# Layer 3's parameters in ten steps, one a unit; the state's product first in its output tile; attention begins beside the first sequence's parameters

## The chip, the core and the metric

The kernel runs on one core of a Trainium2 chip. A core has engines that each work through their own queue in order: TensorE (PE; its weight loads are shown apart as PEld), VectorE (DVE), ScalarE (ACT), GpSimd (POOL) and SyncE (SP). Matrix products go from SBUF into PSUM, from where VectorE and ScalarE read them. The metric is the time of one execution on the device in microseconds (us). Times are stated as medians over runs, and the profile shows one execution.

## The reference

The program is a stack of four layers on x of shape (8, 512, 128). Each layer computes `x = x + s * silu(g)`, with an "attention" part s and a "feed-forward" part g, both of the normalized x. Only layer 3 is changed. Its s is a state-space mixer with rotary angles, and its g an attention of 16 heads of width 8 whose softmax runs over the queries:

```python
xn = _layernorm(x, axis=-1)
# s: state-space mixer
z, x, Bg, Cg, dd_dt, dd_A, trap, angles = split(u @ W_in)
a = jnp.minimum(-softplus(dd_A), -A_FLOOR)
dt = softplus(dd_dt + dt_bias)
theta = jnp.cumsum(angles[:, :, None, :] * dt[..., None], axis=1)
K = _rope(_rmsnorm(Bg, B_norm_w)[:, :, None, :] + B_bias, theta)
Q = _rope(_rmsnorm(Cg, C_norm_w)[:, :, None, :] + C_bias, theta)
...
y = (y_intra + y_inter) + D[None, None, :, None] * x
s = (y * silu(z)).reshape(b, L, D_INNER) @ W_out
# g: attention
scores = jnp.einsum('bqd,bkd->bkq', q, k) / jnp.sqrt(D)
attn = jax.nn.softmax(scores, axis=-1)
z = _l2_normalize(jnp.einsum('bkq,bkv->bqv', attn, v) @ Wo)
g = gelu(_l2_normalize(z @ Wff))
x = x + s * silu(g)
```

`y_intra` is what a chunk of the sequence gives to itself, `y_inter` what the state before the chunk gives to it.

## The kernel before

Layer 3 works on 8 sequences of 512 tokens, each in JT = 4 tiles of 128 tokens. All of a sequence's work is written as Python generators, each `yield` ending one step:

- `begin(b)`: layernorm, transposed tokens xT, the projections kT, qT, V, and then `parameters`.
- `parameters(q)`: B, C, dt, decay, angles and so on for the whole sequence. It holds the products L1743 to L1747, two tanh, `softplus` (a chain of some 15 small VectorE operations on 128x32 elements, L1608 to L1620), the decay's sums L1777 with their exponentials L1779, the norm of B and C (`rms` and L1789), their dot products, and theta (L1808 and L1810) with its reduction to one turn and sine and cosine (L1815 to L1828).
- `mixer(b, jt)`: one tile of the state-space mixer: z and x (L1838), rotation (L1852 to L1854), decay matrix E (L1859, L1864), transposes of B and C into kqT (L1878, copied out by L120 on ScalarE or L122 on VectorE in turn), their products (L1883) times E (L1884), the new state (L1889 to L1895), then the output tile `py` with both halves: the chunk's own product (L1900), read by VectorE at L1901, and the state's (L1904), read at L1906. The sum times z (L1909) is transposed into `yT` (L1913).
- `scores(b, u)`: one unit, four heads by 128 keys: four products into four PSUM banks `pu` (L1946), four maxima on VectorE (L1949), four exponentials with their sums on ScalarE (L1950). `weigh(b, u)`, two units later (LAG = 2), scales the values (L1923, and L1924 on POOL) and adds the products up in one bank `pf` (L1931).
- `end(b)`: W_out's product s (L1959), Wo's product z (L1969), the norms, Wff (L1985), Gelu, the gate and the output's DMA (L1997).

`layer3` sets the order. `begin(0)` runs to its end first. Then follow 8 x 16 units and LAG more; in each unit `scores` and `weigh` are emitted with higher priority (AHEAD = 300), and every generator that is running makes one step, half of them between `scores` and `weigh`. `begin(b + 1)` starts with sequence b's unit 0, a mixer four units ahead of the unit with its number (HEAD = 4), `end(b)` right after the last weigh.

TensorE's instructions keep the order in which they are written (`manual_schedule`). Those of the other engines are ordered by a scheduler, by priority and readiness, when the program is built; each engine then runs its own in that order. All products but scores and weigh go through a ring of three PSUM tiles `pa`. A tile may be written anew when all that read its last contents are done, and a tile is tracked as a whole: a write to one half of `py` waits for reads of the other.

Of the kernel before, what the change touches and what calls it, by code (L numbers as in the profile page):

```python
# [10 lines left out]
F32 = mybir.dt.float32  # L11
# [9 lines left out]
P = 128  # L21
B = 8
T = 512
C = 128
N = B * T
NT = N // P
JT = T // P
H = 16
LAG = 2
# [1533 lines left out]
HM, HP = 4, 64  # L1563
# [40 lines left out]
def softplus(nc, pool, x):  # L1604

    shape = list(x.shape)
    tl = lambda name: pool.tile(shape, F32, name=name)
    e, z, q, p = tl("sp_e"), tl("sp_z"), tl("sp_q"), tl("sp_p")  # L1608
    nc.scalar.activation(e, x, AF.Abs)
    nc.scalar.activation(e, e, AF.Exp, scale=-1.0)  # L1610
    nc.vector.tensor_scalar(z, e, 2.0, None, ALU.add)
    nc.vector.reciprocal(z, z)
    nc.vector.tensor_tensor(z, z, e, ALU.mult)
    nc.vector.tensor_tensor(q, z, z, ALU.mult)
    nc.vector.tensor_scalar(p, q, 1.0 / 17, None, ALU.mult)
    for n in range(15, 1, -2):
        nc.vector.scalar_tensor_tensor(p, p, 1.0 / n, q, ALU.add, ALU.mult)
    nc.vector.scalar_tensor_tensor(p, p, 1.0, z, ALU.add, ALU.mult)
    nc.vector.tensor_scalar(x, x, 0.0, None, ALU.max)
    nc.vector.scalar_tensor_tensor(x, p, 2.0, x, ALU.mult, ALU.add)  # L1620


class Layer3:
# [69 lines left out]
    def begin(self, b):  # L1693
# [32 lines left out]
        q["oT"] = tp.tile([P, 4, T], F32, name="oT3", bufs=1)  # L1726
        q["held"], q["po"] = {}, {}
        yield
        yield from self.parameters(q)

    def parameters(self, q):
# [20 lines left out]

        beta = sm("beta3", 2, JT, HM)
        nc.scalar.activation(beta[:, 0], par[:, :, 8:12], AF.Tanh, scale=0.5)
# [47 lines left out]

        nc.vector.tensor_tensor(v["coef"], v["coef"], kqd, ALU.mult)
# [23 lines left out]
        nc.scalar.activation(n, n, AF.Square)  # L1827
        nc.vector.tensor_scalar(of(cos), n, -2.0, 1.0, ALU.mult, ALU.add)  # L1828
        q.update(v=v, BC=BC, sin=sin, cos=cos, state=None)
        q["yT"] = tp.tile([P, 2, JT, P], F32, name="yT3", bufs=1)  # L1830

    def mixer(self, b, jt):

# [62 lines left out]
            q["state"] = new  # L1896
        yield
        py = k.pa((P, 2, HM, HP))
        for h in range(HM):
            nc.tensor.matmul(py[:, 0, h, :], E[:, h, :], xc[:, h, :], start=True, stop=True)  # L1900
        nc.vector.tensor_tensor(y, y, py[:, 0], ALU.add)  # L1901
        if state is not None:
            for h in range(HM):
                nc.tensor.matmul(py[:, 1, h, :], kqT[:, 1, h, :], state[:, h, :], start=True, stop=True)  # L1904
# [12 lines left out]
    def weigh(self, b, u):  # L1917
# [34 lines left out]
    def end(self, b):  # L1952

        k, nc, cn, fn, tp, q = self.k, self.k.nc, self.cn, self.fn, self.tp, self.q.pop(b)
        s = tp.tile([P, JT, C], F32, name="s3", bufs=1)
        ps = k.pa((P, JT, C))
        for jt in range(JT):
            for w in range(2):
                nc.tensor.matmul(  # L1959
                    ps[:, jt, :], q["yT"][:, w, jt, :], cn["W_out"][:, w * C : (w + 1) * C],  # L1960
                    start=(w == 0), stop=(w == 1),
                )
        nc.scalar.copy(s, ps)
        yield
        z = tp.tile([P, JT, C], F32, name="zo3", bufs=1)
        ps = k.pa((P, JT, C))
        for qt in range(JT):
# [4 lines left out]
                )  # L1972
        nc.scalar.copy(z, ps)
        yield
        r = self.rms(z, JT, 1e-12, floor=True)
        nc.vector.tensor_tensor(z, z, bc(r, 2, C), ALU.mult)
        yield
# [23 lines left out]
def layer3(k, x, A, at):  # L2001

    with ExitStack() as ctx:
        ctx.enter_context(k.banks("l3p", pu=4, pf=1, pa=3))
        L = Layer3(k, ctx, x, A, at, k.out)
        ctx.enter_context(k.tc.manual_schedule(engines={mybir.EngineType.PE}))
        for _ in L.begin(0):
            pass
        U = 4 * JT
        AHEAD = 300  # L2010
        HEAD = 4
        running = [L.mixer(0, 0)]
        for n in range(B * U + LAG):
            b, u = divmod(n, U)
            steps = iter(running)

            def step(share):

                for _ in range(share):
                    w = next(steps, None)  # L2020
                    if w is not None and next(w, False) is False:
                        running.remove(w)

            if b < B:
                if u == 0 and b + 1 < B:
                    running.append(L.begin(b + 1))
                mb, mu = divmod(n + HEAD, U)
                if mb < B and mu % 4 == 0 and (mb, mu) != (0, 0):
                    running.append(L.mixer(mb, mu // 4))
                steps = iter(list(running))  # L2030
                half = (len(running) + 1) // 2
                with k.tc.high_priority(offset=AHEAD):
                    L.scores(b, u)
                step(half)
            else:
                half = 0
            if n >= LAG:
                wb, wu = divmod(n - LAG, U)
                with k.tc.high_priority(offset=AHEAD):
                    L.weigh(wb, wu)  # L2040
                if wu == U - 1:
                    running.insert(0, L.end(wb))
            step(len(running))
        while running:
            for w in list(running):
                if next(w, False) is False:
# [87 lines left out]
```

## Time and profile before

| | us |
|---|---|
| median of 3 timed runs (lowest, highest) | 3675.19 (3669.09, 3679.26) |
| the profiled execution's own time | 3659.7 |
| its span, first to last instruction | 3658.0 |
| first and last start of a reduction L1949 | 2689.6 and 3630.0 |

Layer 3's constants are loaded at 2646.5 us, so it takes the last 1011 us of the span. Start of the first reduction of each sequence's unit 0, from the trace: 2689.6, 2813.8, 2935.5, 3055.6, 3178.1, 3296.4, 3416.9 and 3534.1 us, that is 117 to 124 us a sequence, and 94 for the last up to its last exponential.

The page gives each engine's busy time, share of the span and instructions, and then the span in 40 slices (91 us each), one digit for the busy tenths of each:

```profile
PE 2812.2 (77%) x16390; PEld 1510.1 (41%) x16390; DVE 2265.6 (62%) x6274; ACT 1643.1 (45%) x3211; POOL 783.7 (21%) x915
...
PE   6164657512988888699999999998668789887987
...
DVE  7989898997581121334445445444467777777775
ACT  5163546512544445233333333333245566666665
...
PEclk8585757555899999799998998998878899888987
```

The last eleven slices are layer 3. PEclk is the TensorE clock that was granted, in tenths of full speed. Of the costliest groups, these belong to layer 3 (line, engine, operation, out<-in with shapes, count; busy us and mean ns of one; idle time of the engine just before, and what ended it):

```profile
L1950 ACT ACTIVATE at<-pu,nm 128x512 f32<-128x512 f32 x512 | 347.7, 687 | 145.9 <-DVE nm L1949 115.6
...
L1949 DVE TENSOR_REDUCE nm<-pu 128x1 f32<-128x512 f32 x512 | 326.4, 679 | 66.8 <-PE pu L1946 66.7
...
L1946 PE MATMUL pu<-qT,kT 32*128 32x512 f32 x1024 | 247.6, 700 | 6.4 <-ACT at L1950 5.4
```

A matmul of this kind is recorded as two instructions, and four matmuls on different rows of the array run at once.

### The profile page before, as it was taken

How to read it: one execution, taken by the hardware profiler on the slowest of the kernel's cores; microseconds unless marked ns; L12 is line 12 of the kernel's file. 1: busy time of each engine (PE TensorE's matmuls, PEld its weight loads, DVE VectorE, ACT ScalarE, POOL GpSimd, SP SyncE). 2: the span in 40 equal slices, each digit the busy share in tenths (PEclk: the TensorE clock that was granted, in tenths of full speed). 3: DMA queues.
4: the chain of work that ended last, by engine and by line, in shares of the span. 5: the costliest groups of instructions: out<-in, count | busy, mean ns of one | idle time of the engine just before them, and what ended most of it. 6: DMA issues, size and time to landing. Idle time of an engine off the chain costs nothing.

```text
span 3658.0 us, 45079 instructions
## 1 busy us (share of the span) xinstructions
PE 2812.2 (77%) x16390; PEld 1510.1 (41%) x16390; DVE 2265.6 (62%) x6274; ACT 1643.1 (45%) x3211; POOL 783.7 (21%) x915
## 2 busy tenths in 40 slices
PE   6164657512988888699999999998668789887987
PEld 4142445302444444344444444444344445444543
DVE  7989898997581121334445445444467777777775
ACT  5163546512544445233333333333245566666665
POOL 0004040400226664201101101101122222222220
PEclk8585757555899999799998998998878899888987
DMA  4002030311002221100000000000000000000000
GB/s 119 2 2 71 1 81 1 72 48 34 1 10 45 38 38 24 58 1 1 1 1 1 1 1 1 1 1 1 18 3 1 4 4 1 4 4 4 1 4 6
DMA packets 67519, 64.53 MB, mean 18 GB/s; under 512 B 5344, under 2 KB 59616, under 8 KB 66784
## 3 DMA queue, kind: packets, MB, share of 16 engines
q1 hardware_dynamic: 39264, 42.75, 3.7%
q0 software_dynamic: 19712, 14.69, 2.9%
q10 hardware_dynamic: 8320, 4.19, 0.4%
q8 instruction: 129, 2.11, 0.2%
q14 instruction: 94, 0.77, 0.1%
HBM read 43.80 MB, written 17.83 MB: 17 GB/s over the span
## 4 chain that ended last, share of the span: by engine, by line
PE 45%; DVE 32%; ACT 13%; POOL 4%; issue 3%; DMA 1%; ACTq 0%; POOLq 0%; SPq 0%; DVEq 0%
PE pa L1361 6%; PE pu L1379 6%; DVE nm L1949 4%; ACT at L1950 4%; PE pu L1066 2%; PE pf L1086 2%; PE pu L1946 2%; DVE mpad L1393 2%; PE pf L1424 2%; DVE Z L700 2%; PE pf L1931 1%; PE pa L1475 1%; PE pa L1474 1%; PE pa L1000 1%; DVE Z L706 1%
## 5 line engine op out<-in xcount | busy, mean ns | idle before, releaser
L1950 ACT ACTIVATE at<-pu,nm 128x512 f32<-128x512 f32 x512 | 347.7, 687 | 145.9 <-DVE nm L1949 115.6
L199 POOL TENSOR_SCALAR_AFFINE_SELECT at<-at 128x512 f32<-128x512 f32 x256 | 187.2, 751 | 1030.4 <-ACT at L1411 856.9
L1949 DVE TENSOR_REDUCE nm<-pu 128x1 f32<-128x512 f32 x512 | 326.4, 679 | 66.8 <-PE pu L1946 66.7
L1393 DVE TENSOR_REDUCE mpad<-pu 128x2 f32<-128x256 f32 (+3 forms) x256 | 199.0, 817 | 169.1 <-PE pu L1390 169.1
L1411 ACT ACTIVATE at<-pu 128x1024 f32<-128x1024 f32 (+3 forms) x256 | 171.6, 701 | 286.3 <-PE pu L1379 286.1
L1071 ACT ACTIVATE at<-pu,rsqrt 128x1024 f32<-128x1024 f32 (+3 forms) x256 | 190.4, 791 | 225.3 <-PE pu L1066 221.8
L1946 PE MATMUL pu<-qT,kT 32*128 32x512 f32 x1024 | 247.6, 700 | 6.4 <-ACT at L1950 5.4
L1361 PE MATMUL pa<-hid,f 128*128 128x512 f32 x512 | 222.7, 593 | 0.0
L1379 PE MATMUL pu<-qT,kT 32*128 32x512 f32 (+3 forms) x1024 | 161.4, 518 | 56.5 <-DVE mpad L1393 41.8
L748 PE MATMUL pa<-ident,Y 128*128 128x128 f32 x32 | 7.9, 424 | 216.3 <-DVE Y L739 216.3
L1379 PE MATMUL pu<-kT,qT 32*128 32x128 f32 (+3 forms) x1024 | 152.1, 571 | 14.3 <-ACT at L1411 10.2
L548 POOL DMA_INDIRECT xg<-xn_d,idx x48 | 53.1, 1106 | 503.9 <-PE pf L552 321.8
L1931 PE MATMUL pf<-at,va 128*32 128x512 f32 x1024 | 156.4, 687 | 1.4 <-POOL va L1924 1.4
L1361 PEld LDWEIGHTS pa<-hid,f 128*128 128x128 f32 x512 | 96.6, 190 | 119.5 <-issue 118.9
L1086 PE MATMUL pf<-at,va 128*32 128x512 f32 (+3 forms) x1024 | 106.1, 490 | 42.1 <-POOL at L199 41.8
L1482 DVE SCALAR_TENSOR_TENSOR X<-X,u 128x512 f32<-128x512 f32 x56 | 38.6, 690 | 159.5 <-ACT u L1477 159.5
L1066 PE MATMUL pu<-qT,kT 32*128 32x512 f32 (+3 forms) x1024 | 130.5, 520 | 5.9 <-ACT at L1071 4.9
L1924 POOL TENSOR_TENSOR va<-V,sm 128x32 f32<-128x32 f32 x128 | 38.4, 300 | 450.4 <-DVE sm L1923 399.7
L1379 PEld LDWEIGHTS pu<-qT,kT 32*128 32x128 f32 x1024 | 67.8, 198 | 155.1 <-DVE mpad L1393 115.6
L1946 PEld LDWEIGHTS pu<-qT,kT 32*128 32x128 f32 x1024 | 82.2, 208 | 103.2 <-ACT at L1950 65.5
L1009 POOL DMA_INDIRECT f_d<-ys,idx x64 | 101.2, 1582 | 95.7 <-DMA f_d<-ys,idx 51.4
L1362 ACT ACTIVATE hid<-pa,f 128x512 f32<-128x512 f32 x64 | 44.0, 687 | 172.6 <-PE pa L1361 172.6
(608 smaller groups left out, 6606.4 us busy)
## 6 DMA issues: line engine op xcount, KB each, us to landing
w<-in_w_dram SPq DMA_DIRECT2D x24, 512.0 KB, 3.3
f_d<-zeros ACTq DMA_DIRECT2D x8, 512.0 KB, 6.0
xn_d<-xn SPq DMA_DIRECT2D x8, 512.0 KB, 3.6
w<-in_w_dram SPq DMA_DIRECT2D x16, 256.0 KB, 2.8
w<-in_w_dram SPq DMA_DIRECT2D x24, 128.0 KB, 2.1
f<-in_f_dram SPq DMA_DIRECT2D x1, 2888.0 KB, 11.8
xn<-in_x_dram SPq DMA_DIRECT2D x4, 512.0 KB, 7.5
Gt<-in_x_dram SPq DMA_DIRECT2D x4, 512.0 KB, 3.9
```

The costliest lines, as they stand in the source:

```text
L199: self.nc.gpsimd.affine_select(a, a if src is None else src, pattern, ALU.is_ge, 0.0, base=0, channel_multiplier=-1)
L1066: nc.tensor.matmul(pu[:, n, 0:m], q["kT"][r, g // 2, kc * P : kc * P + P], q["qT"][r, g, kc * P :], start=True, stop=True,)
L1071: nc.scalar.activation(at_[:, i : i + 2, 0:m], pu[:, :, 0:m], AF.Square, bias=k.rsqrt2, scale=32.0**-0.5)
L1086: nc.tensor.matmul(po[i * 32 : i * 32 + 32, kc * P :], va[:, kc, c0 : c0 + 32], at_[:, i, 0 : T - kc * P], start=(kc == 0), stop=(kc == JT ...
L1361: nc.tensor.matmul(ps, fn[n][:, c0 : c0 + P], src[:, i, :], start=(i == 0), stop=(i == 3))
L1379: self.k.nc.tensor.matmul(pu[:, n, 0:m], a[r, c0 : c0 + P], b[r, q0 : q0 + m], start=True, stop=stop)
L1393: nc.vector.tensor_reduce(top[:, i : i + 2, 16], pu[:, :, 0:m], AX.X, ALU.max)
L1411: nc.scalar.activation(at_[:, i : i + 2, 0:m], pu[:, :, 0:m], AF.Exp, scale=8.0**-0.5)
L1931: nc.tensor.matmul(po[i * 32 : i * 32 + 32, :], va[:, kc, c0 : c0 + 32], E[:, i, :], start=(kc == 0), stop=(kc == JT - 1))
L1946: nc.tensor.matmul(pu, q["kT"][r, kc * P : (kc + 1) * P], q["qT"][r, g, :], start=True, stop=True)
L1949: nc.vector.tensor_reduce(nm[:, w], pu, AX.X, ALU.max, negate=True)
L1950: nc.scalar.activation(E[:, n, :], pu, AF.Exp, bias=nm[:, w], accum_out=sm[:, w])
```

## The change

Line numbers in all texts are those of the kernel before, but for the changed lines' own. The change does this:

- `softplus` becomes a generator with a step after its first two operations, and `parameters` gets more steps, so that it makes ten from its first product on. The norm's `rms` is written before softplus instead of after the decay's exponentials. `yT` is taken by a sequence's first mixer.
- In `mixer`, the state's product is written before the chunk's own, and VectorE's reads follow both.
- In `end`, z (Wo) comes first, and s (W_out) follows in the next step, once the sequence's last mixer is done.
- `layer3` runs `begin(0)` only until q, k and V are made, and starts the units then; in the first six, every running generator makes a second step. Mixers start one unit before the unit with their number, but not before unit 6 and then every third. `begin(1)` starts at unit 2, and each `end` a unit later than before.

```diff
@@ softplus
     nc.scalar.activation(e, e, AF.Exp, scale=-1.0)
+    yield
     nc.vector.tensor_scalar(z, e, 2.0, None, ALU.add)
@@ begin
         yield
+        q["ready"] = True
         yield from self.parameters(q)
@@ parameters
             if jt % 2:
                 yield
+        r = self.rms(raw.rearrange("p j a n -> p (j a) n"), 2 * JT, 1e-5)
...
-        softplus(nc, self.sp2, sp.rearrange("p a b c -> p (a b c)"))
+        yield from softplus(nc, self.sp2, sp.rearrange("p a b c -> p (a b c)"))
+        yield
...
         nc.vector.tensor_tensor(v["eout"], v["eout"], v["c"], ALU.mult)
-
-        r = self.rms(raw.rearrange("p j a n -> p (j a) n"), 2 * JT, 1e-5)
+        yield
...
+            if jt == 1:
+                yield
+        yield
         prod = ap.tile([P, JT, C], F32, name="prod3")
...
         nc.vector.tensor_tensor(v["coef"], bc(cn["D"], 1, JT), v["coef"], ALU.subtract)
+        yield
...
-        q["yT"] = tp.tile([P, 2, JT, P], F32, name="yT3", bufs=1)
@@ mixer
         py = k.pa((P, 2, HM, HP))
+        if state is not None:
+            for h in range(HM):
+                nc.tensor.matmul(py[:, 1, h, :], kqT[:, 1, h, :], state[:, h, :], start=True, stop=True)
         for h in range(HM):
             nc.tensor.matmul(py[:, 0, h, :], E[:, h, :], xc[:, h, :], start=True, stop=True)
         nc.vector.tensor_tensor(y, y, py[:, 0], ALU.add)
         if state is not None:
-            for h in range(HM):
-                nc.tensor.matmul(py[:, 1, h, :], kqT[:, 1, h, :], state[:, h, :], start=True, stop=True)
             inter = tl("inter3", HM, HP)
...
+        if jt == 0:
+            q["yT"] = self.tp.tile([P, 2, JT, P], F32, name="yT3", bufs=1)
...
+        q["mixed"] = jt
         yield
@@ end: z's product and copy moved up, then
+        yield
+        while q.get("mixed") != JT - 1:
+            yield
         s = tp.tile([P, JT, C], F32, name="s3", bufs=1)
@@ layer3
-        for _ in L.begin(0):
-            pass
...
-        HEAD = 4
-        running = [L.mixer(0, 0)]
...
+        EARLY, EVERY = 6, 3
+        at = lambda b, jt: max(b * U + jt * JT - 1, EARLY + EVERY * (b * JT + jt))
...
+        for b in range(B):
+            if b:
+                read = at(b - 2, JT - 1) + 1 if b > 1 else 0
+                plan(max((b - 1) * U, at(b, 0) - U, read), lambda b=b: L.begin(b))
+            for jt in range(JT):
+                plan(at(b, jt), lambda b=b, jt=jt: L.mixer(b, jt))
+            plan((b + 1) * U + LAG, lambda b=b: L.end(b))
+        running = [L.begin(0)]
+        while not L.q or "ready" not in L.q[0]:
+            next(running[0])
+        for n in range(B * U + LAG + 1):
+            running.extend(make() for make in work.get(n, ()))
...
+            if n < EARLY:
+                step_all = list(running)
+                for w in step_all:
+                    if next(w, False) is False:
+                        running.remove(w)
```

More of the change, by code (lines that the diff above doesn't have):

```diff
@@ L1954, in end @@
         k, nc, cn, fn, tp, q = self.k, self.k.nc, self.cn, self.fn, self.tp, self.q.pop(b)
[L1955 to L1964, printed above, removed]
         z = tp.tile([P, JT, C], F32, name="zo3", bufs=1)
@@ L1974, in end @@
         yield
+        while q.get("mixed") != JT - 1:
+            yield
+        s = tp.tile([P, JT, C], F32, name="s3", bufs=1)
+        ps = k.pa((P, JT, C))
+        for jt in range(JT):
+            for w in range(2):
+                nc.tensor.matmul(
+                    ps[:, jt, :], q["yT"][:, w, jt, :], cn["W_out"][:, w * C : (w + 1) * C],
+                    start=(w == 0), stop=(w == 1),
+                )
+        nc.scalar.copy(s, ps)
         r = self.rms(z, JT, 1e-12, floor=True)
@@ L2006, in layer3, with plan @@
         ctx.enter_context(k.tc.manual_schedule(engines={mybir.EngineType.PE}))
-        for _ in L.begin(0):
-            pass
         U = 4 * JT
         AHEAD = 300
-        HEAD = 4
-        running = [L.mixer(0, 0)]
-        for n in range(B * U + LAG):
-            b, u = divmod(n, U)
-            steps = iter(running)
+        EARLY, EVERY = 6, 3
+        at = lambda b, jt: max(b * U + jt * JT - 1, EARLY + EVERY * (b * JT + jt))
+        work = {}
+        def plan(n, make):
+            work.setdefault(n, []).append(make)
@@ new lines, in layer3 @@
+        for b in range(B):
+            if b:
+                read = at(b - 2, JT - 1) + 1 if b > 1 else 0
+                plan(max((b - 1) * U, at(b, 0) - U, read), lambda b=b: L.begin(b))
+            for jt in range(JT):
+                plan(at(b, jt), lambda b=b, jt=jt: L.mixer(b, jt))
[5 more added lines that the diff above has]
+            running.extend(make() for make in work.get(n, ()))
+            todo = list(running)
@@ L2017, in step @@
             def step(share):
-                for _ in range(share):
-                    w = next(steps, None)
-                    if w is not None and next(w, False) is False:
+                for w in todo[:share]:
+                    if next(w, False) is False:
                         running.remove(w)
[L2024 to L2031, printed above, removed]
-                with k.tc.high_priority(offset=AHEAD):
[L2033 to L2036, printed above, removed]
@@ L2037, in layer3 @@
-            if n >= LAG:
-                wb, wu = divmod(n - LAG, U)
-                with k.tc.high_priority(offset=AHEAD):
[L2040 to L2043, printed above, removed]
+                del todo[:share]
+            if n < B * U:
+                with k.tc.high_priority(offset=AHEAD):
+                    L.scores(*divmod(n, U))
+                step((len(todo) + 1) // 2)
+            if LAG <= n < B * U + LAG:
+                with k.tc.high_priority(offset=AHEAD):
+                    L.weigh(*divmod(n - LAG, U))
@@ L2044, in layer3 @@
+            step(len(todo))
+            if n < EARLY:
+                step_all = list(running)
+                for w in step_all:
+                    if next(w, False) is False:
+                        running.remove(w)
         while running:
```

## The prediction

> **What bounds the kernel now.** The change touches layer 3 alone, so I read the stretch from 2647 us (its constants are issued at 2646.5) to the end, first as busy time by stretch. Its 128 units of attention (a unit is one `scores` call, four VectorE reductions L1949 and four ScalarE exponentials L1950) fall into eight sequences of 16. The columns after the stretch and its length are busy time and instructions of each engine, the granted TensorE clock, and DMA.
>
> ```profile
> core 0: us, PE busy (x) PEld busy (x) DVE busy (x) ACT busy (x) POOL busy (x), PEclk, DMA share, GB/s
> 2647.00:2690.00 43.00, 17.82 (x67) 11.83 (x68) 26.14 (x79) 8.32 (x19) 10.11 (x10) 0.64 0.12 44
> ...
> 2936.00:3056.00 120.00, 100.51 (x563) 54.19 (x562) 89.54 (x212) 76.73 (x196) 27.00 (x41) 0.89 0.01 3
> ...
> 3534.00:3630.00 96.00, 87.05 (x485) 44.67 (x488) 65.06 (x132) 59.18 (x160) 17.67 (x31) 0.88 0.01 4
> ```
>
> Row one is the head: 43 us in which no unit starts. Row two is a full sequence with the next one's `begin` beside it, row three the last, which has none. TensorE is the busiest engine of both, but 20 of 120 us idle. So I ask what TensorE waited for, over 2690 to 3634 us.
>
> ```profile
> engine line waited for: us in total, times, longest us
> PE pa L1904 <- DVE y L1901: 50.6, 24, 3.3
> PE pa L1883 <- DVE coef L1803: 40.8, 3, 13.6
> PE pa L1838 <- DVE angle L1818: 28.1, 3, 9.8
> ```
>
> Three causes hold 119.5 of the 147 us that TensorE stood idle there. The first is the state's product, which goes into the same output tile `py` as the product before it, and waits for VectorE to have read that one. It comes three times in every sequence. The timeline shows one:
>
> ```profile
> 2851.70 1.10 PE L1900 MATMUL pa<-xc,E 128*128 128x64 f32 x8
> ...
> 2855.23 1.78 PE L1904 MATMUL pa<-state,kqT 128*128 128x64 f32 x8 [2.42 <-DVE y L1901]
> ...
> 2856.80 2.02 PE L1859 MATMUL pa<-upto,adt 128*128 128x128 f32 x8
> ...
> 2858.75 2.09 PE L1946 MATMUL pu<-qT,kT 32*128 32x512 f32 x8
> ```
>
> The other two come once a sequence. The wait put down to `coef` stands here, beside what VectorE did in it:
>
> ```profile
> 2885.81 0.68 DVE L122 COPY kqT<-pa 128x512 f32<-128x512 f32 x1
> 2886.41 0.16 DVE L1803 TENSOR_TENSOR coef<-coef,kqd 128x16 f32<-128x16 f32 x1
> ```
>
> ```profile
> 2886.63 2.05 PE L1883 MATMUL pa<-kqT 128*128 128x128 f32 x8 [13.61 <-DVE coef L1803]
> ```
>
> L1883 reads kqT, so what it needed was the copy that ended just before. That copy stood behind the last part of `parameters` on VectorE (BC, prod, dot, turns, angle, and pieces of `end`), which is emitted in one step with no reduction of a later unit between. The angle wait is the same block seen through the ring of three `pa` tiles: theta's tile is free only when L1818 has read it. That unit lasts 20.0 us (first reductions at 2874.9 and 2894.9) where light units take about 4.
>
> **The change, part by part.** It removes no arithmetic. The built program has as many TensorE instructions as before; they and the work on VectorE and ScalarE move.
>
> *State's product first.* Both products are written before VectorE reads, so the 24 waits go: -50.6 us. Here the clock matters. The Trainium skill (TensorE: Matmul & The Clock Gate, HAM oscillation) warns of idle gaps over some 3.4 us; by that rule a gap of 2.4 us costs only itself, and this part is worth 50.6. The row says otherwise:
>
> ```profile
> 2855.50:2862.30 6.80, 6.80 (x32) 4.46 (x35) 3.61 (x13) 1.79 (x6) 0.64 (x1) 0.50 0.00 0
> ```
>
> The clock is 0.50 for 6.8 us after that gap. L1904 took 1.78 against 1.10 of L1900 with the same shape, L1859 2.02 against 1.16 (eight such products of L1883 at full clock), L1946 2.09 against 1.14: 2.5 us more a time, 60 us over 24. By the row the part is worth 50.6 to 111. I count a quarter, -15, because at full speed TensorE would need less than VectorE and ScalarE in many of those units and would wait for them.
>
> *Parameters in steps.* The block waits sum to 75.7 us: 40.8 and 28.1 above, 4.6 at L1777 behind adt in sequence 0, 2.2 at L1883 behind ScalarE's copy. In the order of the changed program I summed VectorE's work between the reductions of two units, each line at its mean duration of before. Before, one unit a sequence carries 16 to 20 us. After, none from sequence 2 on carries over 9.2, and the sum per sequence stays (97 to 100). TensorE's dependants move with it: theta's products now stand after the reductions that precede their readers. Below zero the part can't go, as the work is the same; at best all 75.7 goes. VectorE still has units of 7 to 9 us where TensorE has 6 to 7, so I leave a quarter: -57. The squares of `raw` (1.06 us ScalarE, then a reduction of 1.22 and POOL's power of 1.63) go ahead of softplus, off any wait that TensorE shows: 0.
>
> *Mixers later, and a wait added.* Mixers start three units later in the steady state and every three units at first. In one mixer of each of sequences 1 to 7, and in the last, the changed order has L1909 (y times z) behind the four reductions of the unit after which TensorE wants to transpose y; before, L1909 was always a unit ahead. Behind the transposes in TensorE's queue stand the next weigh and scores, for which ScalarE waits. Price: four reductions, 2.48 us where they run together, 8 times: +20. Its ends are 0 (transposes a little late hide it) and 40 (with the slow clock after, as above).
>
> *The head.* First scores can start when qT is made, 2664.3 us. Now they wait:
>
> ```profile
> 2682.62 0.14 DVE c L1772
> ...
> 2688.51 0.02 issue
> 2688.54 0.70 DVE turns L1815
> ```
>
> (the chain of waits: start, length, what.) The first reduction is at 2689.6. After the change, units 0 to 5 run beside this chain. VectorE then has 21 of its 26.1 us in the head still to do, some 4 for the angle, and 24 reductions of 0.64 (15): 40 us, so unit 6 begins near 2706 and not at 2743.5. But before, two mixers (9.35 us of TensorE each, from the busy time of its eight lines over 32 mixers) were nearly done by then, which are now caught up: 37 - 16 = 21 gained. Two lumps remain in VectorE's new order (17 us before unit 3's reductions, 14.5 before unit 8's). Ends: 0 and 24 (2689.6 less 2665).
>
> *ScalarE.* The changed order has 44 table loads in the layer against 40, at 1.28 us: +5 at most, since Sin stands between exponentials.
>
> *The tail.* Wo's product (3.74 us) goes ahead of W_out's (2.05), which then lies beside the norm; but the last mixer ends two units nearer to it: -1, ends -2 and +2. Output DMAs stay in SyncE's order, eight as before; none is issued earlier than its sequence's end, and layer 3 moves at most 4 GB/s after its head, so no queue is passed that could hurt.
>
> **Sum.** -50.6 - 15 - 57 + 20 - 21 + 5 - 1 = -119.6 us. Against the profiled span, 3658.0 becomes 3538.4, or 3540 with the 1.7 us outside it (3659.7). The median of the timed runs is 15.5 above that execution, 3675.2; the same difference gives **3556 us**.
>
> **Rivals.**
> *Everything is gained.* 50.6 + 60 + 75.7 + 24 + 2 - 5 = 207, so 3468. For it: from 2800 to 2855 us, where nothing stalls, TensorE was busy 51.65 of 55 at clock 0.97. Against: VectorE has 89.5 and ScalarE 76.7 us of work in a sequence, so 120 can't become 92. About half way, 3515, is the most I expect.
> *The waits move.* The slices bring each its own small wait, at L1909, at adt, at theta's tile. Half of the block waits stay (+38 for my 57 becoming 38 gained, so +19), the added wait costs its 40 (+20), and the head gives 5 (+16): -119.6 + 55 = -65, so 3611. For it: adt and theta still stand directly behind reductions in VectorE's order, in the unit in which TensorE asks.
> *Slower: every slice is exposed.* VectorE is in order, so each of nine slices (about 2.2 us of the 20) can delay reductions, hence ScalarE, hence the next scores, and a gap of that size halves the clock as at 2855 us: 2.2 + 2.5 = 4.7 each, 9 x 7 sequences x 4.7 = 296, against 50.6 + 15 + 75.7 + 21 = 162 gained: +134, 3809. It decides once over 55% of the slices are exposed. Against: scores are put 300 ahead in priority, and light units run at 4.1 us with VectorE busy only 2.5 of them.
> *It doesn't do what it says.* The scheduler could keep the block whole; its order shows that it doesn't after sequence 1.
>
> **Chances and range.** Forecast with its unknown costs (3515 to 3595) 0.72; waits move (3595 to 3655) 0.15; everything gained (below 3515) 0.06; slower or nothing 0.07. A change under 0.3% (11 us) can't be told from none. Cutting a tenth at each side: 3505 to 3615. Faster 0.93, within 0.3% 0.02, slower 0.05.
>
> **What would show it.** Right: the state's product shows no wait for y; the sequences' length is near 106 us; no unit over 12 us after sequence 1; the first reduction near 2667; the granted clock of the layer above 0.92. Wrong: the transposes of y (L1913) wait over 3 us many times, half-clock stretches as long as before (270 of 949 us), or units 0 to 5 that last over 50 us together.

## The result, and the profile after

| | time, us (median, lowest to highest) | ratio, 95% interval |
|---|---|---|
| before, runs alongside | 3677.23 (3669.09 to 3679.79) | 1 |
| after | 3647.91 (3643.43 to 3650.08) | 0.9921 (0.9904 to 0.9937) |
| forecast | 3556 (3505 to 3615) | |

The change gains 29 us where 120 were forecast. First the page of the changed kernel: busy time, and the three groups of attention (busy us and mean ns; then idle time ahead, and what ended it). The lines of before that answer to these are L1950, L1949 and L1946.

```profile
PE 2827.7 (78%) x16390; PEld 1510.2 (41%) x16390; DVE 2283.3 (63%) x6274; ACT 1648.0 (45%) x3215; POOL 782.7 (21%) x915
...
L1961 ACT ACTIVATE at<-pu,nm 128x512 f32<-128x512 f32 x512 | 347.5, 687 | 150.8 <-DVE nm L1960 138.9
...
L1960 DVE TENSOR_REDUCE nm<-pu 128x1 f32<-128x512 f32 x512 | 325.8, 681 | 65.0 <-PE pu L1957 65.0
...
L1957 PE MATMUL pu<-qT,kT 32*128 32x512 f32 x1024 | 253.6, 699 | 16.1 <-ACT at L1961 15.6
```

Busy time by stretch of the changed kernel (columns as in the prediction): the first sequence, two neighbours in the steady state, the last.

```profile
core 0: us, PE busy (x) PEld busy (x) DVE busy (x) ACT busy (x) POOL busy (x), PEclk, DMA share, GB/s
2678.50:2808.90 130.40, 95.11 (x437) 45.15 (x437) 96.04 (x246) 74.73 (x195) 25.77 (x37) 0.75 0.00 1
3054.40:3168.50 114.10, 104.94 (x563) 56.46 (x563) 88.92 (x202) 73.64 (x192) 26.97 (x40) 0.85 0.01 3
3168.50:3291.30 122.80, 102.13 (x563) 55.11 (x563) 94.69 (x219) 78.78 (x201) 26.90 (x40) 0.83 0.01 3
3526.80:3620.00 93.20, 85.01 (x504) 44.79 (x506) 67.90 (x133) 62.42 (x169) 19.52 (x34) 0.91 0.01 4
```

The first sequence lasts 130.4 us and the other full ones 112.7 to 124.9, against 117 to 124 before. TensorE idles a little less, but its clock is lower. Over all eight sequences, first before, then after:

```profile
2689.60:3631.70 942.10, 794.53 (x4366) 430.08 (x4366) 689.72 (x1612) 587.68 (x1528) 206.59 (x310) 0.86 0.01 3
```

```profile
2678.50:3620.10 941.60, 803.92 (x4374) 428.60 (x4374) 720.32 (x1659) 594.98 (x1543) 210.74 (x314) 0.84 0.01 3
```

What TensorE waited for in layer 3 of the changed kernel (total us, times, longest):

```profile
PE pa L1890 <- ACT kqT L120: 20.0, 3, 7.2
PE pa L1781 <- DVE adt L1772: 18.9, 3, 13.1
...
PE pa L1982 <- DVE E L1891: 14.8, 5, 3.0
PE pa L1781 <- DVE c L1776: 14.8, 1, 14.8
PE pa L1923 <- DVE y L1917: 10.8, 5, 5.0
PE pa L1885 <- DVE sm L1934: 8.8, 2, 4.4
```

The three waits that the prediction built on are gone: no wait for y at the state's product (now L1908), none for coef at the kqT products (L1890), none for the angle at L1845. Others stand in their place. Among them are two that the prediction had in its 75.7 us of block waits as small ones: adt at the decay's sums (L1781, before L1777) grew from 4.6 to 18.9 us, and ScalarE's copy of kqT from 2.2 to 20.0.

To compare versions I measure layer 3 from the start of the last product with `ff_w1` in layer 2 (L1498). The layers ahead of that point have the same source in every version, yet lasted from 2639.5 to 2656.2 us in the profiled executions (2641.9 before, 2655.4 after). The next table leaves them out; the verdicts rest on ratios to runs of the kernel before that were made alongside. "Head" ends at the first reduction, "sequences" run to the last exponential. Idle, gaps and half-clock time are TensorE's in the sequences (gaps of at least 0.3 us in the sum, of at least 1.5 us in the count); half-clock time is the time in us for which the granted clock was 0.5.

| version | ratio | head | sequences | idle | gaps | half clock |
|---|---|---|---|---|---|---|
| before | 1 | 47.7 | 942.1 | 146 | 31 | 270 |
| after | 0.9921 | 23.1 | 941.6 | 136 | 29 | 300 |
| a1_state_first | 0.9834 | 47.7 | 880.8 | 109 | 17 | 208 |
| a2_no_state_first | 1.0071 | 23.1 | 990.0 | 178 | 41 | 331 |
| a3_late_start | 0.9932 | 47.7 | 917.0 | 116 | 28 | 273 |
| a4_few_steps | 0.9938 | 23.1 | 943.3 | 163 | 28 | 263 |
| b1_few_late_mix4 | 0.9788 | 47.7 | 872.3 | 98 | 11 | 191 |
| b2_state_first_end | 0.9876 | 47.7 | 896.4 | 119 | 25 | 229 |
| b3_mix3 | 0.9877 | 23.1 | 915.2 | 141 | 31 | 242 |
| b4_state_first_steps | 0.9899 | 47.7 | 902.7 | 122 | 23 | 218 |
| c1_one_sine | 0.9878 | 23.1 | 936.3 | 124 | 29 | 297 |
| c2_steps_one_sine | 0.9803 | 47.8 | 875.2 | 83 | 21 | 215 |
| c3_mix4_one_sine | 0.9748 | 47.7 | 860.9 | 92 | 9 | 177 |
| c4_mix3_one_sine | 0.9840 | 23.1 | 921.9 | 148 | 31 | 253 |
| d1_mix4_cuts_one_sine | 0.9825 | 47.7 | 879.0 | 80 | 15 | 229 |
| d2_state_one_sine | 0.9783 | 47.8 | 867.5 | 98 | 16 | 174 |
| d3_few_early_mix4 | 0.9876 | 23.1 | 924.2 | 130 | 18 | 256 |
| d4_zo_pool | 0.9870 | 23.1 | 917.7 | 120 | 23 | 266 |
| e1_zo_pool_one_sine | 0.9838 | 23.1 | 903.8 | 112 | 28 | 236 |
| e2_mix4_one_cut | 0.9774 | 47.7 | 859.1 | 81 | 13 | 167 |

Intervals are plus or minus 0.0013 to 0.0017; 0.001 is 3.7 us. The trace columns come from one execution each. In all versions but c1 to c4, what layer 3 (with the 24 to 28 us after the last exponential) gained in the trace agrees with the ratio within 7 us; in those four the ratio shows 6 to 14 us more, so differences to c1, c2 and c3 are given by the trace too where they matter. Rows one and two are the result: the layer gained 24.6 us in its head, and the eight sequences together are as long as before.

### The profile page after: what moved, and what is told of

Its sections match the earlier page's. It is cut to its first block, busy times and chain, and to the rows that moved or that the text cites. A ratio compares the mean times of both kernels' runs of the same rounds, so it can differ in the third digit from the quotient of the medians.

```text
span 3647.1 us, 45081 instructions
## 1 busy us (share of the span) xinstructions
PE 2827.7 (78%) x16390; PEld 1510.2 (41%) x16390; DVE 2283.3 (63%) x6274; ACT 1648.0 (45%) x3215; POOL 782.7 (21%) x915
## 4 chain that ended last, share of the span: by engine, by line
PE 38%; DVE 14%; ACT 7%; POOL 3%; issue 3%; DMA 1%; POOLq 0%; ACTq 0%; DVEq 0%; SPq 0%
PE pa L1361 6%; PE pu L1379 6%; PE pu L1957 3%; ACT at L1961 3%; DVE nm L1960 3%; PE pf L1942 2%; DVE mpad L1393 2%; PE pf L1424 2%; PE pa L1475 1%; PE pa L1474 1%; ACT at L1411 1%; PE pa L1498 1%; PE pa L1348 1%; POOL rs L1691 1%; PE pu L1066 1%
## 5 line engine op out<-in xcount | busy, mean ns | idle before, releaser
L1942 PE MATMUL pf<-at,va 128*32 128x512 f32 x1024 | 164.9, 722 | 0.7 <-DVE oT L122 0.7
```

Of the source, the lines that this page charges most:

```text
L1942: nc.tensor.matmul(po[i * 32 : i * 32 + 32, :], va[:, kc, c0 : c0 + 32], E[:, i, :], start=(kc == 0), stop=(kc == JT - 1))
```

## The experiments

**First question: which part brings what?**

a1, the kernel before with only this:

```diff
+        if state is not None:
+            for h in range(HM):
+                nc.tensor.matmul(py[:, 1, h, :], kqT[:, 1, h, :], state[:, h, :], start=True, stop=True)
         for h in range(HM):
             nc.tensor.matmul(py[:, 0, h, :], E[:, h, :], xc[:, h, :], start=True, stop=True)
         nc.vector.tensor_tensor(y, y, py[:, 0], ALU.add)
         if state is not None:
-            for h in range(HM):
-                nc.tensor.matmul(py[:, 1, h, :], kqT[:, 1, h, :], state[:, h, :], start=True, stop=True)
```

> The kernel before with one edit: in each mixer the state's product is written ahead of the chunk's own. Theory A (my forecast: TensorE's waits are on the path): 50 to 66 us faster than before, ratio 0.982 to 0.986. Theory B (the waits move: a unit's chain of scores, reductions, exponentials over in-order queues sets the pace, and a wait taken off TensorE comes back as another): 0 to 20 us faster, ratio 0.995 to 1.000, with TensorE's idle time in the layer down by less than 25 us of the 50.

a2, the changed kernel with that edit undone:

> The changed kernel with that one edit undone. Theory A: 50 to 66 us slower than the changed kernel (3648), that is 3700 to 3715. Theory B: within 15 us of it, 3645 to 3663.

a3, the changed kernel with the first sequence begun whole, and no catching up:

```diff
-        while not L.q or "ready" not in L.q[0]:
-            next(running[0])
+        for _ in running.pop():
+            pass
-        EARLY, EVERY = 6, 3
-        at = lambda b, jt: max(b * U + jt * JT - 1, EARLY + EVERY * (b * JT + jt))
+        EARLY = 0
+        at = lambda b, jt: max(b * U + jt * JT - 1, 0)
```

> The changed kernel, but the first sequence's parameters run to their end before the first unit, and mixers stand one unit ahead from the start, with no catching up. If the early start brings what its first reduction shows (24.7 us earlier against the layer's start): 15 to 25 us slower than the changed kernel, 3663 to 3673. If the first two sequences give it back (they took 130.4 and 124.9 us, against 124.2 and 121.7 before): within 8 us of 3648, or faster.

a4, the changed kernel with its six new `yield`s in `parameters` taken out:

> The changed kernel with the steps of the parameters put together again (the same steps as before, all else as changed). Theory A: 40 to 57 us slower than the changed kernel, 3690 to 3705. Theory B: 0 to 25 us slower, 3648 to 3673, since the 20 us block on VectorE comes back in one unit while light units and ScalarE had slack around it.

Measured: a1 3609.03 us, 0.9834 (0.9821 to 0.9848); a2 3696.01, 1.0071 (1.0057 to 1.0085); a3 3644.37, 0.9932 (0.9918 to 0.9945); a4 3648.45, 0.9938 (0.9925 to 0.9952). The state's product is worth 0.0166 alone (61 us) and 0.0150 in the changed kernel (55 us). a2 lies between its two forecasts. The early start and the six cuts each stay within the intervals of no effect. Everything but the state's product therefore costs 0.0087, 32 us, together.

The traces say what the six cuts did. In a4, without them, TensorE waited 89.2 us for the parameters at L1781; in the changed kernel it is 39.6 (18.9, 14.8 and 5.9).

```profile
PE pa L1781 <- DVE adt L1772: 59.3, 6, 11.1
PE pa L1781 <- DVE c L1776: 29.9, 2, 16.8
```

So the cuts took away 49.6 us of these waits. But TensorE's idle time fell by 27 only, since others came, such as the 20.0 for kqT, of which a4 has none at those products; and the half-clock time rose by 37.

**Second question: what costs 32 us: the mixers' place, the order of `end`, or the cuts?**

b1, from a4: late start as in a3, and mixers four units ahead as before the change:

```diff
-        at = lambda b, jt: max(b * U + jt * JT - 1, EARLY + EVERY * (b * JT + jt))
+        at = lambda b, jt: max(b * U + jt * JT - 4, 0)
```

> The changed kernel with the old few steps of the parameters, the first sequence begun whole before the first unit, and every block's mixer begun four units ahead of its first unit, as in the kernel before; the new loop, the new order of the end and the earlier mean squares stay. It differs from the version with only the state's product first (3609.0 us) by the end's order and the loop alone. If the mixers' place is what costs the changed kernel its 39 us against that version: 3605 to 3616. If the end's order (W_out's products after Wo's, a unit later) is: 3630 to 3648. If the cost is the steps': 3605 to 3616 too, and the version with steps tells these two apart.

b2, from a1: only the new order in `end` (Wo's product first, W_out's behind it):

> The kernel before with the state's product first and the new order of the end, nothing else. If the end's order costs (the five waits of 2.97 us for VectorE at W_out's products, seen in the changed kernel, and the slow clock behind them): 3625 to 3640. If the end is neutral: 3605 to 3614, as with the state's product alone (3609.0).

b3, the changed kernel with `- 3` for `- 1` in that line:

> The changed kernel with each mixer from the second sequence on begun three units ahead instead of one; all else as changed (3648). If the mixers' place against the parameters' steps costs the 39 us: 3612 to 3630. If it is the end's order or the steps themselves: 3640 to 3652.

b4, from a1: three of the six cuts (two about the softplus, one ahead of `prod`), and a second `yield` behind `v["c"]`, where one stood already. That one isn't among the six of the change: it puts the products of L1777 one step later. The expectations call them "four of the six".

> The kernel before with the state's product first and four of the six new cuts in the parameters (two about the softplus, one ahead of the cumulative products, one behind B and C's scaling; with all six they would not be done when the next mixer starts at four units ahead). By the forecast, in which every sequence's stalls over parameters go: 3565 to 3580. If cuts help only the first two sequences and lose in the others (as few steps against ten, 3648.5 against 3647.9, said): 3600 to 3614. If the steps themselves are what costs: 3630 to 3645.

Measured: b1 3595.19 us, 0.9788; b2 3626.33, 0.9876; b3 3626.20, 0.9877; b4 3634.13, 0.9899. b2, b3 and b4 each came out where its part had been expected to cost, so none of the three stands alone. In the layout of before, the four cuts cost 24 us and the new `end` 15; in the changed kernel, mixers two units earlier bring 16 back. b1 came out lower than any of its expectations. None of the theories so far says why cuts, which only spread work, should cost. The units that have become long say more.

**What the long units show.** In the changed kernel the last unit of sequence 2 lasts 15.5 us. Its timeline (start, length, engine, line, tiles), ScalarE and TensorE alone:

```profile
3038.78 1.28 ACT L1833 ACT_TABLE_LOAD   x1
3038.81 1.25 PE L1957 MATMUL pu<-qT,kT 32*128 32x512 f32 x2 [0.21 <-ACT at L1961]
3040.07 0.63 ACT L1833 ACTIVATE sin<-angle 128x512 f32<-128x512 f32 x1
3040.72 1.28 ACT L1961 ACT_TABLE_LOAD   x1
3042.01 0.69 ACT L1961 ACTIVATE at<-pu,nm 128x512 f32<-128x512 f32 x1
...
3044.82 1.28 ACT L1834 ACT_TABLE_LOAD   x1
3046.11 0.63 ACT L1834 ACTIVATE turns<-angle 128x512 f32<-128x512 f32 x1
3046.65 0.57 ACT L120 COPY kqT<-pa 128x512 f32<-128x512 f32 x1
3047.11 0.63 ACT L1835 ACTIVATE turns<-turns 128x512 f32<-128x512 f32 x1
3047.27 2.08 PE L1890 MATMUL pa<-kqT 128*128 128x128 f32 x8 [7.21 <-ACT kqT L120]
3047.76 1.28 ACT L1848 ACT_TABLE_LOAD   x1
```

ScalarE loads the sine's table, takes one sine, goes back for four exponentials, loads the sine's table again for the half angle, and only then copies kqT, for which TensorE has waited 7.21 us with the next weigh and scores behind it. The loads in layer 3 are 44, as the prediction counted from the order; the pair of sines is split by exponentials in six of eight sequences. But it was split in four of eight before, and is in seven in a4, which lacks the cuts and has no such wait for kqT: what a split costs depends on what stands behind it.

In unit 3 of sequence 3 something else happens. Its timeline:

```profile
3076.51 1.02 POOL L1691 TENSOR_TENSOR rs<-ss,minus_half 128x4 f32<-128x4 f32 x1 [7.49 <-DVE ss L1687]
...
3077.50 2.00 POOL L1854 TENSOR_TENSOR kq<-BC,c 128x1024 f32<-128x1024 f32 x1
3077.56 2.48 DVE L1988 TENSOR_TENSOR zo<-zo,rs 128x512 f32<-128x512 f32 x1 [0.54 <-POOL rs L1691]
...
3079.96 0.68 DVE L1891 TENSOR_TENSOR E<-E,pa 128x512 f32<-128x512 f32 x1
...
3080.69 3.64 PE L1982 MATMUL pa<-c,yT 128*128 128x128 f32 x16 [2.97 <-DVE E L1891]
```

GpSimd's addition for the next mixer (L1854) starts 0.06 us ahead of VectorE's scaling of Wo's output. The scaling takes 2.48 us, where the same instruction takes 0.69 in all eight sequences of before; it ends 0.54 us after GpSimd does. The product E stands behind it on VectorE, and TensorE idles for 2.97 us until that product has read its tile. The 16 products with W_out then run at half clock, 3.64 us; the unit lasts 12.4. Six of the eight scalings in the changed kernel take 2.48 us, in a3 seven; with mixers three or four units ahead (b1, b3, d3) all take 0.69. With mixers one unit ahead, mixer and `end` meet in one unit. The Trainium skill (SBUF — State Buffer, Who interferes with whom) has the rule: a VectorE instruction with two inputs in SBUF and a GpSimd instruction that reads SBUF share a port pair that is locked, and the later one waits for the whole of the earlier. The row agrees: 1.94 us of waiting and 0.54 of work.

This is no cost of the cuts: a2 has six such scalings, and so has a4, which lacks the cuts. Nor is it what the new `end` costs in b2, whose eight scalings all take 0.69.

**Third question: are the split sines the cost of the cuts?** c1 is the changed kernel, c2 is b4, c3 is b1 and c4 is b3, each with one activation for both sines:

```diff
-        t = ap.tile([P, W], F32, name="angle3")
+        tt = ap.tile([P, 2, W], F32, name="angle3")
+        t = tt[:, 0]
...
-        nc.scalar.activation(of(sin), t, AF.Sin)
-        nc.scalar.activation(n, t, AF.Sin, scale=0.5)
+        nc.vector.tensor_scalar(tt[:, 1], t, 0.5, None, ALU.mult)
+        sc = tp.tile([P, 2, W], F32, name="sin3")
+        nc.scalar.activation(sc.rearrange("p a w -> p (a w)"), tt.rearrange("p a w -> p (a w)"), AF.Sin)
```

> The changed kernel, but the angle and its half stand side by side and one activation takes the sine of both, so that no exponential of the scores can come between the two sines and ScalarE loads its tables once less each way. In the changed kernel every sequence but two has exponentials between its sines (loads of the sine's table twice per sequence), and the unit in which this falls lasts 13 to 15.5 us against 6 to 8 beside it. If the split pair is what the cuts cost (theory S): seven sequences by 4 to 6 us, so 3605 to 3620. If the cost is the mixers' place or the end alone: 3640 to 3650.

> The version with the state's product first and four cuts in the parameters in the old loop (3634.1 us, all its sequences with a split pair, units of 12.1 to 13.7 us), with the one activation for both sines. Theory S: the cuts lose only through the split pair, so 3595 to 3610, at or under the version without cuts (3609.0, three of eight sequences split). If the cuts lose by where they put the other work: 3625 to 3635.

> The fastest version so far (few steps, late start, mixers four units ahead; 3595.2 us), with one activation for both sines. Only its first two sequences have a split pair. Theory S: 3588 to 3596, two splits' worth at most. If one activation is worth something of itself (one more VectorE multiplication against one ScalarE instruction less per sequence): another 1 us a sequence either way, 3585 to 3603.

> The changed kernel with mixers three units ahead (3626.2 us), with the one activation. Its even sequences have split pairs and last 122.1, 120.7 and 115.4 us, its odd ones have none and last 110.5 and 108.4. Theory S: the even ones come down to the odd ones' length, so 3 by 7 to 11 us and the first two by some: 3595 to 3608. If the even sequences are longer for another reason: 3618 to 3626.

Measured: c1 3627.28 us, 0.9878 (0.9863 to 0.9893); c2 3597.52, 0.9803; c3 3577.53, 0.9748 (0.9732 to 0.9763); c4 3612.53, 0.9840. All four gain by the ratios, c2 by 0.0096 (35 us; 28 by the trace), c3 by 0.0040 and the changed kernel by 0.0043 (16 us). Only 6 of the 16 are in the trace of layer 3 (985.5 us for 991.7); the rest is in the layers ahead, and I don't count on it. Only c2 came out as the theory of the split pair (S) expects. c1 stays above its 3605 to 3620. c3 lies below everything expected of it, though only two of its pairs had been split; in the trace its layer is 11.6 us shorter than b1's. c4 doesn't follow the theory at all: in its trace the even sequences stayed at 116 to 120 us and the odd ones rose to 113, so its layer 3 is no shorter than b3's. Where the waits for kqT went, c1 shows:

```profile
PE pa L1924 <- DVE y L1918: 27.9, 10, 5.4
```

The wait for y at the transposes was 10.8 us in the changed kernel. One wait had covered another.

**Fourth question: cuts without split sines, the mixers' place alone, the collision alone.** d1 is c3 with the four added `yield`s of b4; d2 is a1 with one activation for both sines; d3 is a4 with `- 4` for `- 1`. d4 is the changed kernel with

```diff
-        nc.vector.tensor_tensor(z, z, bc(r, 2, C), ALU.mult)
+        nc.gpsimd.tensor_tensor(z, z, bc(r, 2, C), ALU.mult)
```

> The fastest version so far (few steps, late start, mixers four units ahead, one activation for the sines; 3577.5 us) with four of the six new cuts in the parameters. Its five or six waits of 8.6 us each for the parameters' chain on VectorE, and units of 16 to 17 us around them, are what the cuts are there to take away. If cuts do their work once the sines are not split: five waits by 8.6 us, 3535 to 3562. If the work only moves to other units: 3570 to 3585.

> The kernel before with the state's product first and one activation for both sines, no cuts: the control for the version with cuts (3597.5 us). If the cuts are worth something of themselves there: 3600 to 3609, that is above 3597.5. If they are worth nothing: 3592 to 3600, and then one activation is worth 10 to 17 us without any cut. If they still cost: under 3592.

> The changed kernel with the old few steps (3648.5 us), and each mixer from the second sequence on four units ahead instead of one; the early start stays. It differs from the version of 3595.2 us by the early start alone. If the mixers' place is the cause: 3590 to 3604. If the late start was half of that version's gain: 3615 to 3630.

> The changed kernel (3647.9 us), but the scaling of Wo's output by its root mean square runs on GpSimd instead of VectorE, ahead of the addition that it collided with (2.48 us instead of 0.69, and 2.97 us of TensorE waiting for the product behind it, five times, in the unit that lasts 12.5 us). If that collision is how the mixers' place costs: the five waits go with 3 to 4 us of slow clock behind each, 3620 to 3634. If the unit is long for the work that it holds: 3642 to 3652.

Measured: d1 3599.48 us, 0.9825 (0.9812 to 0.9839); d2 3584.67, 0.9783; d3 3616.81, 0.9876; d4 3615.66, 0.9870 (0.9855 to 0.9885). Runs of before were 8 us lower on this chip than on the last one, so the ratios count, not the expected times. d4 measures the collision: 0.0051 (19 us) by moving one instruction, which also takes its eight times 0.69 us off VectorE. The same unit of d4:

```profile
3059.48 0.68 DVE L1891 TENSOR_TENSOR E<-E,pa 128x512 f32<-128x512 f32 x1
3060.15 1.04 POOL L1988 TENSOR_TENSOR zo<-zo,rs 128x512 f32<-128x512 f32 x1
...
3060.22 2.05 PE L1982 MATMUL pa<-c,yT 128*128 128x128 f32 x16
```

The wait of 2.97 us is gone, the W_out products run at full clock, and the unit lasts 9.3 us. d3 gains 0.0062 (23 us) by the mixers' place and b3 16. Neither has a scaling of 2.48 us, so the collision can be most of what the mixers' place costs; no run has the place changed without it. And d3 against b1, which starts late, shows that the early start can cost: 0.0088, 32 us.

d1 is the plainest against the forecast. Once the sines can't be split, the four cuts still cost 0.0077 (28 us; 18 by the trace) against c3, and 0.0020 (7 us, with overlapping intervals) in c2 against d2. What TensorE waited for, first in c3, then in d1:

```profile
PE pa L1781 <- DVE kqd L1802: 26.8, 3, 8.9
PE pa L1781 <- DVE adt L1772: 18.2, 2, 9.1
```

```profile
PE pa L1921 <- DVE y L1915: 21.7, 7, 5.4
PE pa L1888 <- ACT kqT L120: 17.7, 3, 6.0
```

The waits for the parameters are gone from d1, as the cuts were meant to do, and others have come. Idle time falls by 12 us. But the gaps of 1.5 us and more rise from 9 to 15 and the half-clock time by 52 us, which is 26 us more than the same work at full clock: 26 - 12 = 14, where the sequences lengthen by 18.

It is tempting to say that each new gap slows the clock behind it, but the traces don't show that. In the changed kernel, 13 of 37 half-clock stretches begin although TensorE idled less than 0.5 us in the 3.4 us ahead (the shortest such stretch on record); in c3 it is 14 of 23, in d1 18 of 35. One of the changed kernel, with the stretch ahead of it:

```profile
2858.70:2865.50 6.80, 6.80 (x39) 4.27 (x36) 6.80 (x22) 4.43 (x13) 2.81 (x5) 1.00 0.01 2
2865.70:2872.40 6.70, 6.70 (x28) 3.90 (x28) 6.70 (x16) 3.18 (x9) 1.58 (x2) 0.50 0.00 0
```

TensorE counts as busy for all of both, and the clock halves between them. So more half-clock time goes with the cuts, and why it does stays open.

**Fifth question: do the two repairs add up, and does one more step pay right ahead of the wait?** e1 is the changed kernel with d4's edit and c1's. e2 is c3 with one `yield` behind `v["c"]`, ahead of L1781.

> The changed kernel with both repairs: Wo's output scaled on GpSimd, and one activation for both sines. The changed kernel is 0.9921 of the kernel before, the repairs alone 0.9870 and 0.9878. If they are separate costs, their gains add: 0.9827 plus or minus 0.0015 (3598 to 3609 against 3668), at the level of the state's product alone. If another wait takes the place of the one removed: 0.985 to 0.987.

> The fastest version (0.9748 of the kernel before; few steps, late start, mixers four units ahead, one activation for the sines) with one cut, ahead of the cumulative products, where TensorE waits 8.6 to 9.1 us for VectorE in each of six sequences. If a cut pays where it stands right ahead of the wait: six waits by 6 to 9 us and the slow clock behind them, 0.960 to 0.968. If VectorE's parameters' chain is late by the same amount at whatever comes next: 0.973 to 0.978.

Measured: e1 3600.80 us, 0.9838 (0.9824 to 0.9851); e2 3577.87, 0.9774 (0.9761 to 0.9788). The repairs together gain 0.0083 where their sum is 0.0094: two separate costs, additive within the intervals. e2 doesn't pay. The line that answers to c3's above:

```profile
PE pa L1782 <- DVE par L1801: 28.0, 6, 5.2
```

TensorE asks a unit later, and VectorE's chain is late there too, by 4.7 us a time for 8.6 to 9.1. Its sequences are 1.8 us shorter in the trace, and the timed runs show no gain. The fastest version by the ratio is c3, 0.9748, 93 us under before; in the traces e2's layer is as short (932.0 us against 933.2). c3 has the state's product first, the new `end` and loop, the few old steps, the late start, mixers four units ahead, and one activation for the sines.

## Why the prediction was wrong

| step of the sum | forecast, us | what the runs showed |
|---|---|---|
| state's product first | -50.6 - 15 | -61 alone, -55 in the changed kernel |
| parameters in steps | -57 | -6 (after against a4, intervals overlap); +24, +7 and +28 for the four cuts elsewhere |
| wait for y at the transposes | +20 | 20.2 us of waits at L1923 in the trace, 10.8 of them put down to y; no run prices it |
| head | -21 | -4 by the ratios, 0 by the traces (a3); +32 in d3 against b1 |
| table loads | +5 | four more, as counted; removing all six split pairs gains 6 by the trace, 16 by the ratio (c1), but four were split before too |
| tail | -1 | 26.3 us before, 27.0 after |
| VectorE blocked by GpSimd | not in the sum | 19 (d4) |

- **The state's product was right in size and in its two causes, with some luck in the split.** The 24 waits went, but idle time fell by 37 us and not by 50.6, as waits for kqT (17.7) and xv (12.4) came in a1; half-clock time fell by 62 us, which is worth 31 and not the 15 allowed. The rule that the prediction weighed would have given 50.6; its own quarter on top of the row with clock 0.50 gave 65.6; 61 was measured.
- **The step that failed is "so I leave a quarter: -57".** It takes three quarters of the block waits as time gained. The cuts did take 49.6 us of waits for the parameters away (a4 against the changed kernel), close to 57, but the time fell by 6. Other waits came, so that idle time fell by 27, and half-clock time rose by 37, worth 18. The same was seen in other layouts: half-clock time rose by 10 (a1 to b4), 41 (d2 to c2) and 52 us (c3 to d1), and gaps of 1.5 us and more rose from 17 to 23, 16 to 21 and 9 to 15. The prediction had counted VectorE's work between reductions, in which no unit carried over 9.2 us from sequence 2 on, and took the rest as hidden; it had not asked what the moved steps fall beside on ScalarE and TensorE. Why the clock was lower more of the time stays open.
- **The head failed as a term**, not as an event. The first reduction comes 23.1 us into the layer instead of 47.7, about as forecast. But the first two sequences last 130.4 and 124.9 us, against 112.2 and 114.2 in a3: 28.9 us given back for 24.6. In the changed kernel TensorE waits 14.79 us in sequence 0 at L1781 for the first parameters, with the scores queued behind. I had priced the mixers to be caught up by TensorE's time, and not by the wait for the parameters that they all share.
- **Of the signs I named**, two came out right: no wait for y at the state's product, and the first reduction 23.1 us into the layer (near 2667 on before's axis, which is 25). Sequences of 106 us, no unit over 12 after sequence 1 and a clock over 0.92 did not: 112.7 to 130.4, up to 15.5, and 0.84. Of the failing ones, half-clock time grew (270 to 300 us). Units 0 to 5 last 55.4 us together, but lasted 53.9 before, so that sign could not tell; waits over 3 us at the transposes of y came, but not many times.
- **The rival "waits move" named the mechanism**, at 3611, and was too mild. Most of the missing 90 us is in two terms: 51 of the 57 for the steps, 17 or more of the 21 for the head. The collision (19) comes on top of them, and is a cost of the mixers' place beside `end`, which the prediction had not put into its sum. The terms were measured in different layouts, so the column doesn't add up exactly to the 29 measured.

What stays open: with both repairs the changed kernel (e1) is still 0.0055 above d2, 20 us. Its trace has 36.8 us of waits at the transposes of y, and longer first sequences; no run separated these. Nor did a run show why b1, with the new `end` and loop, is 0.0046 (17 us) under a1, while `end` alone (b2) is 0.0042 over it.

## What to carry to other kernels

Waits that go are not yet time gained. Cutting a long block into slices took 50 us of waits away here and gained 6 at most: count gaps and half-clock time beside the waits, since one gap of 9 us a sequence cost less here than waits of 3 to 6 us. When a step is moved, look at what it falls beside on every engine: which activations it puts between two that share a table, and which GpSimd instruction starts just ahead of a VectorE instruction with two inputs in SBUF (19 us here). Run the parts of such a change one at a time: here one of them held the whole gain, and the rest cost half of it.

## What the runs showed of the hardware

- TensorE's clock fell to half behind gaps under 3 us: 2.42 us in the row of before that the prediction shows, 2.97 us ahead of W_out's products in the changed kernel. It also fell where TensorE had been busy for 6.80 of 6.80 us (row above), so gaps alone don't explain it. Across the twenty profiled versions the sequences' length is idle time plus half of the half-clock time plus 646 to 695 us, worked out from the table; idle time is 80 to 178 us of it and half of the half-clock time 84 to 166, so the clock is as large a term as the waits.
- A VectorE multiplication of 0.69 us took 2.48 beside a GpSimd addition of 2.00 that had started 0.06 us earlier, the same in each of the six sequences.
- A change of tables on ScalarE took 1.28 us, and the next activation started 0.01 us later; the sine itself took 0.63. In the changed kernel a copy of kqT queued behind a split pair, and TensorE waited 7.21 us for it.
